# A depthwise convolution's last channel chunk for two more images, computed by ScalarE and GpSimd, and one store of three issued by GpSimd

## The chip, the cores and the metric

The kernel runs on one core of a Trainium2 chip. A core has five engines with an instruction queue each, which run side by side and wait for one another through semaphores: TensorE (PE in the profile; PEld is its weight load) multiplies matrices into PSUM, VectorE (DVE) and ScalarE (ACT) do elementwise work, GpSimd (POOL) does elementwise work on SBUF, and SyncE (SP) only issues transfers. A transfer can be issued by SP, ACT or POOL; it stands in that engine's queue, in order, with everything else that the engine does.

The metric is the device time of one execution in microseconds. Before the change it is 3717.47 us, the median of three runs (3716.41 to 3720.61).

## The reference

The network has four residual layers on an image batch of 8 x 384 channels x 32 x 32 pixels in float32. Each layer adds its result to its input, which it first group-normalises (32 groups). The change concerns the first part of layer 0:

```python
def _dwproj(x, dw, g, b, pw):
    C = x.shape[1]
    y = lax.conv_general_dilated(x, dw, (1, 1), ((1, 1), (1, 1)), feature_group_count=C, ...)
    y = jax.nn.gelu(_bn(y, g, b), approximate=False)
    return jnp.einsum('oc,bchw->bohw', pw, y)
...
q = _dwproj(x, dw_q, g_q, b_q, pw_q).reshape(B, heads, hd, N)
k = _dwproj(x, dw_k, g_k, b_k, pw_k).reshape(B, heads, hd, N)
v = _dwproj(x, dw_v, g_v, b_v, pw_v).reshape(B, heads, hd, N)
```

So three depthwise 3 x 3 convolutions are made of every normalised image, one each for q, k and v: every channel is convolved by itself with nine weights. `_bn` takes mean and variance of each convolved channel over the whole batch, so that no image can go on to the attention before all eight are convolved. Then follow the attention of layer 0, a mixture of experts (layer 1), a ternary-weight convolution (layer 2) and a deformable attention (layer 3). The change leaves those alone.

## The kernel before

**Layout.** Channel 3p + c of an image is on partition p in chunk c (KC = 3 chunks of P = 128 partitions), with 1024 pixels along the free dimension.

**Stage A** is the block under `with ExitStack() as pa` (L217 to L449). For each image b:

- `norm(b)` (L248) group-normalises it in three steps, which are put into three successive turns of the work loop. `begin` takes statistics on VectorE (L103) and joins them (L108). `middle` sends a small matmul through TensorE (L114) and copies it back on VectorE (L116). `end` does a second small matmul (L125), VectorE's L127, a power on GpSimd (L95) and VectorE's L130; then ScalarE writes the three normalised chunks into a padded image `pads[b % 2]` (L144). For some images VectorE copies chunk 2 of it to `xn` (L268).
- `stack(b, g)` (L311) builds TensorE's operand for one group of channels. A group has 42 channels, and its tile has 126 rows: each channel three times, shifted by one image row each. SP issues three SBUF-to-SBUF transfers for it (L318). There are nine such groups in an image (three in each chunk), plus one small group of the last six partitions (index NGC).
- The work loop (from L362) takes one group a turn. Six matmuls (in the profile two instructions each, so 12) convolve it for q, k and v at once into two PSUM banks; ScalarE copies each bank to `y` (L397), VectorE takes its batch statistics (L398), and the three parts of `y` are stored to DRAM, one each for q, k and v (L406). ScalarE's queue issues these stores, except those of the last image's groups 5, 6 and 7, which GpSimd's queue issues.

**What is taken off TensorE already.** For the images in `ON_V` (0, 2, 4, 6) the three large groups of chunk 2 are left out of TensorE's work. `convolve(b, xn)` (L275) computes that chunk on VectorE instead: for each of q, k, v a product with the centre weight (L290) and eight multiply-adds (L292), each over the 126 x 961, 992 or 1024 elements that a shift leaves, and then `finish` (L294): two statistics (L297), one 504 KB store on ScalarE's queue (L298) and three small moves of the statistics on SP's (L300). These 30 steps stand in a list `taps`, from which each turn of the work loop takes two.

**The order.** There are 68 turns: 7 for images 0, 2, 4, 6 and 10 for 1, 3, 5, 7. Within a turn the program order is: the norm's step if one is due, the stacks of up to nine turns ahead (AHEAD), the matmuls with their copies and statistics, the three stores, then the two taps. Every engine keeps to this order in its own queue. The turn at which each image's norm begins comes from `begins` (L341); the next image's load is issued there too.

**Buffers.** Images lie in a pool `im` of five slots, taken in rotation. `st` has ten slots, `y` nine (shared by the groups' results and VectorE's products), and PSUM four banks, two for each group.

**After stage A** the batch statistics are joined and turned into scales (to L449), the first image's convolved q, k, v are loaded from DRAM (`load_b(0)`, issued at the last image's group 5), and ScalarE's first gelu (L494) opens the attention.

Of the kernel before, what the change touches and what calls it, by code (L numbers as in the profile page):

```python
# [13 lines left out]
N = H * W  # L14
# [38 lines left out]
def tile_kernel(ctx: ExitStack, tc: tile.TileContext, i: dict, out: bass.AP):  # L53
# [144 lines left out]

    im = ctx.enter_context(tc.tile_pool(name="im", bufs=5))
# [8 lines left out]
    ON_V = (0, 2, 4, 6)  # L208
# [8 lines left out]
    with ExitStack() as pa:  # L217
# [28 lines left out]
        vst = wa.tile([3 * GC, 3, 2, 6], F32, name="vst")  # L246

        def norm(b):  # L248
# [12 lines left out]
            def end():  # L261
# [4 lines left out]
                if b in ON_V:  # L266
                    xn = wa.tile([3 * GC, H, W], F32, tag="xn", name=f"xn{b}", bufs=2)
                    nc.vector.tensor_copy(xn, pads[b % 2][: 3 * GC, KC - 1, 1 : H + 1, :])  # L268
                    taps.extend(convolve(b, xn))
                for c in range(KC):  # L270
                    moments(xmv[:, b, c, :], state["st"][:, 2 * c : 2 * c + 2, :])
# [3 lines left out]
        def convolve(b, xn):  # L275

            state = {}

            def tap(v, t):
                dy, dx = t // 3 - 1, t % 3 - 1  # L280
                w = cwv[: 3 * GC, v, t : t + 1]
                if t == 4:
                    state["y"] = ya.tile([3 * GC, N], F32, tag="y", name=f"yv{b}_{v}")
                y = state["y"].rearrange("p (h w) -> p h w", h=H)
# [4 lines left out]
                if t == 4:  # L289
                    nc.vector.tensor_scalar(d, f, w, None, ALU.mult)  # L290
                else:
                    nc.vector.scalar_tensor_tensor(d, f, w, d, ALU.mult, ALU.add)  # L292

            def finish(v):  # L294
                y = state["y"]
                for h in range(2):
                    nc.vector.bn_stats(vst[:, v, h, :], y[:, h * HALF : (h + 1) * HALF])  # L297
                nc.scalar.dma_start(out=raw[v][b, : 3 * GC, KC - 1, :], in_=y)  # L298
                for t in range(3):
                    nc.sync.dma_start(  # L300
                        out=cst[v : 3 * GC : 3, 3 * (KC - 1) + t, 2 * b : 2 * b + 2, :],
                        in_=vst[t : 3 * GC : 3, v, :, :],
# [3 lines left out]
            for v in range(3):  # L306
                steps += [lambda v=v, t=t: tap(v, t) for t in (4, 0, 1, 2, 3, 5, 6, 7, 8)]
                steps.append(lambda v=v: finish(v))
            return steps
# [26 lines left out]
        groups = [(NGC, *range(NGC - 3 if b in ON_V else NGC)) for b in range(B)]  # L336
# [4 lines left out]
        begins = {max(2, work.index((b, NGC)) - AHEAD - 2): b for b in range(1, B)}  # L341
        sts, taps, todo, later, normed = {}, [], {}, list(work), {0}
# [21 lines left out]
        for n, (b, g) in enumerate(work):  # L364
# [34 lines left out]
            for v in range(3):  # L399
# [5 lines left out]
                queue = nc.gpsimd if b == B - 1 and g in (5, 6, 7) else nc.scalar  # L405
                queue.dma_start(out=to, in_=of)  # L406
            for _ in range(2):
                if taps:
                    taps.pop(0)()
            if b == B - 1:  # L410
# [3 lines left out]
        assert not taps and not todo and not xts  # L414
# [1509 lines left out]
```

## Time and profile before

| | |
|---|---|
| median of three runs | 3717.47 us |
| the profiled execution's own time | 3716.66 us |
| its span, first to last instruction | 3714.9 us |
| PE busy over the span | 3598.4 us (97%) |
| DVE busy | 1810.6 us (49%) |
| ACT busy | 1273.6 us (34%) |
| POOL busy | 195.9 us (5%) |
| first large matmul of stage A starts | 18.0 us |
| last statistics of stage A (L398) end | 384.4 us |
| first gelu of the attention starts (L494) | 390.2 us |
| PE, DVE, ACT, POOL busy from 0 to 385 us | 352.75, 267.86, 105.40, 18.33 us |
| mean granted TensorE clock from 0 to 385 us | 0.96 |

How to read it: a row of the profile names the line, the engine, the operation, and the tile written and read, with shapes and a count. Then come its busy time, the mean of one in ns, the engine's idle time just before such instructions, and what ended that idle time. Instructions that only issue a transfer are not counted as busy, though they hold their queue: ACTq and SPq rows show them. Matmuls overlap in their pipeline, so the mean of one is longer than their spacing.

### The profile page before, as it was taken

How to read it: one execution, taken by the hardware profiler on the slowest of the kernel's cores; microseconds unless marked ns; L12 is line 12 of the kernel's file. 1: busy time of each engine (PE TensorE's matmuls, PEld its weight loads, DVE VectorE, ACT ScalarE, POOL GpSimd, SP SyncE). 2: the span in 40 equal slices, each digit the busy share in tenths (PEclk: the TensorE clock that was granted, in tenths of full speed). 3: DMA queues.
4: the chain of work that ended last, by engine and by line, in shares of the span. 5: the costliest groups of instructions: out<-in, count | busy, mean ns of one | idle time of the engine just before them, and what ended most of it. 6: DMA issues, size and time to landing. Idle time of an engine off the chain costs nothing.

```text
span 3714.9 us, 39037 instructions
## 1 busy us (share of the span) xinstructions
PE 3598.4 (97%) x15587; PEld 1504.2 (40%) x15587; DVE 1810.6 (49%) x2827; ACT 1273.6 (34%) x1524; POOL 195.9 (5%) x162
## 2 busy tenths in 40 slices
PE   7999999999999999999799999999999999999888
PEld 3444333333333333333244444444344444444433
DVE  6776223232323232323336557564764657557564
ACT  2222354545444453544222321323222232322222
POOL 0000100000000000000000010100101010010111
PEclk9999999999999999999899999999999999999898
DMA  6776311121212021212350010110101001010000
GB/s 205 240 249 231 127 55 36 63 56 43 63 40 78 25 75 28 72 28 72 125 201 23 33 51 20 46 42 33 37 23 56 26 33 43 27 51 20 0 34 18
DMA packets 88178, 253.32 MB, mean 68 GB/s; under 512 B 19114, under 2 KB 19706, under 8 KB 87602
## 3 DMA queue, kind: packets, MB, share of 16 engines
q1 hardware_dynamic: 74904, 211.26, 17.1%
q10 hardware_dynamic: 12504, 37.88, 3.0%
q8 instruction: 127, 2.08, 0.2%
q0 software_dynamic: 576, 1.55, 0.1%
q14 instruction: 67, 0.55, 0.0%
HBM read 133.39 MB, written 75.59 MB: 56 GB/s over the span
## 4 chain that ended last, share of the span: by engine, by line
PE 39%; DVE 10%; ACT 1%; issue 1%; DMA 0%; POOL 0%; DVEq 0%; ACTq 0%; POOLq 0%; SPq 0%
PE y L1295 11%; PE ph L1274 8%; DVE y L1370 6%; PE pq L1415 3%; PE pf L1694 3%; PE pw L1378 3%; PE s L1589 3%; PE pav L1605 2%; DVE hd L1260 1%; PE pss L1631 1%; PE pk L1563 1%; PE pv L1572 1%; DVE off L1485 1%; PE xsb L1549 1%; PE px L1438 1%
## 5 line engine op out<-in xcount | busy, mean ns | idle before, releaser
L645 ACT ACTIVATE p<-s 128x1024 f32<-128x1024 f32 x512 | 496.5, 1021 | 507.0 <-PE s L638 506.7
L1295 PE MATMUL y<-hd,w_sb 128*128 128x512 f32 x1080 | 493.1, 600 | 3.5 <-DVE hd L1260 3.5
L653 PE MATMUL pav<-p,vt 64*64 64x512 f32 x4096 | 487.1, 590 | 0.0
L1274 PE MATMUL ph<-h,w_sb 128*128 128x512 f32 x1104 | 484.1, 594 | 0.4 <-DMA w_sb<-in_w_dram 0.4
L638 PE MATMUL s<-qk,qk 48*64 48x512 f32 x3072 | 370.8, 597 | 3.3 <-ACT p L645 3.3
L391 PE MATMUL pk<-st,cw_sb 126*126 126x512 f32 x720 | 320.3, 606 | 12.7 <-DMA st<-pad 10.9
L1274 PEld LDWEIGHTS ph<-h,w_sb 128*128 128x128 f32 x1104 | 207.5, 190 | 259.5 <-issue 255.3
L1295 PEld LDWEIGHTS y<-hd,w_sb 128*128 128x128 f32 x1080 | 198.0, 191 | 248.4 <-issue 238.2
L653 PEld LDWEIGHTS pav<-p,vt 64*64 64x64 f32 x4096 | 156.6, 133 | 285.1 <-issue 285.1
L610 DVE COPY ta<-pav 128x512 f32<-128x512 f32 x64 | 44.3, 692 | 429.0 <-PE pav L653 426.0
L1284 ACT ACTIVATE hd<-ph,b_sb 128x512 f32<-128x512 f32 x180 | 122.6, 681 | 371.3 <-PE ph L1274 371.2
L1370 DVE SCALAR_TENSOR_TENSOR y<-h,tap,y 128x961 f32<-128x961 f32 (+1 forms) x192 | 234.1, 1244 | 0.6
L391 PEld LDWEIGHTS pk<-st,cw_sb 126*126 126x126 f32 x720 | 139.3, 196 | 185.5 <-issue 179.5
L1485 DVE SCALAR_TENSOR_TENSOR off<-q,dw_sb,off 128x225 f32<-128x225 f32 (+3 forms) x432 | 212.3, 549 | 1.7
L638 PEld LDWEIGHTS s<-qk,qk 48*64 48x64 f32 x3072 | 108.7, 133 | 231.1 <-issue 192.0
L78 DVE COPY qk<-pq 128x512 f32<-128x512 f32 x48 | 33.2, 692 | 292.8 <-PE pq L572 292.8
L397 ACT COPY y<-pk 126x512 f32<-126x512 f32 (+1 forms) x136 | 76.2, 583 | 249.2 <-PE pk L391 111.9
L1596 ACT ACTIVATE p<-s 128x1024 f32<-128x1024 f32 x96 | 93.1, 1021 | 169.5 <-PE s L1589 169.4
L1260 DVE TENSOR_TENSOR hd<-hd,cb 128x512 f32<-128x512 f32 x180 | 122.7, 687 | 48.7 <-ACT hd L1284 48.2
L590 PE MATMUL po<-att,wo_sb 128*128 128x512 f32 x288 | 132.8, 615 | 11.6 <-DMA att<-al 11.6
L1378 PE MATMUL pw<-y,upw 128*128 128x512 f32 x288 | 130.5, 606 | 5.0 <-DVE y L1370 5.0
L572 PE MATMUL pq<-g,wq_sb 128*128 128x512 f32 x288 | 131.5, 607 | 2.0 <-ACT g L494 2.0
(286 smaller groups left out, 3870.2 us busy)
## 6 DMA issues: line engine op xcount, KB each, us to landing
g<-raw SPq DMA_DIRECT2D x72, 512.0 KB
st<-pad SPq DMA_DIRECT2D x180, 168.0 KB
raw<-y ACTq DMA_DIRECT2D x171, 168.0 KB
xa<-in_x_dram SPq DMA_DIRECT2D x24, 512.0 KB
xh<-in_x_dram SPq DMA_DIRECT2D x48, 256.0 KB
f<-in_x_dram SPq DMA_DIRECT2D x24, 512.0 KB
f<-o SPq DMA_DIRECT2D x24, 512.0 KB
o<-ot SPq DMA_DIRECT2D x42, 256.0 KB
```

The costliest lines, as they stand in the source:

```text
L391: nc.tensor.matmul(pk[h].rearrange("p (h w) -> p h w", w=W)[: 3 * nch, :, o0 : o0 + c1 - c0], lhsT=lhs, rhs=rhs, start=(k == 0), stop=(k = ...
L572: nc.tensor.matmul(pq, lhsT=w_in[v][:, c, pr * P : (pr + 1) * P], rhs=acts[b][v][:, c, h * HALF : (h + 1) * HALF], start=(c == 0), stop=(c ...
L590: nc.tensor.matmul(po, lhsT=wo0[:, c, m * P : (m + 1) * P], rhs=atts[b][:, c, hs], start=(c == 0), stop=(c == KC - 1),)
L638: nc.tensor.matmul(s[64 * k : 64 * k + 64, j * HALF : (j + 1) * HALF], lhsT=kt[r, k0 : k0 + 64], rhs=qt[r, h * HALF : (h + 1) * HALF], sta ...
L645: nc.scalar.activation(p, s, AF.Exp, scale=scale)
L653: nc.tensor.matmul(pav[k][64 * j : 64 * j + 64, :], lhsT=vts[b % 2][r, kc, 2 * hd : 2 * hd + 2, :].rearrange("p a b -> p (a b)"), rhs=p[r, ...
L1260: nc.vector.tensor_tensor(hd, hd, state["cb"], ALU.mult)
L1274: nc.tensor.matmul(ph, lhsT=w1[:, e, c, dc * P : (dc + 1) * P], rhs=state["h1"][c], start=(c == 0), stop=(c == KC - 1),)
L1295: nc.tensor.matmul(y, lhsT=w2[:, e, dc, m * P : (m + 1) * P], rhs=state[h, k], start=(k == 0), stop=(k == NE * KC - 1),)
L1370: nc.vector.scalar_tensor_tensor(d, f, tap2[:, c, t : t + 1], d, ALU.mult, ALU.add)
L1378: nc.tensor.matmul(pw[h], lhsT=upw2[:, c, m * P : (m + 1) * P], rhs=y[c][:, hs], start=(c == 0), stop=(c == KC - 1),)
L1485: nc.vector.scalar_tensor_tensor(d, f, dw3[:, t : t + 1], d, ALU.mult, ALU.add)
```

## The change

The set `ON_AP` = (1, 3) joins `ON_V`. For images 1 and 3, too, the three large groups of chunk 2 leave TensorE, so that there are 62 turns. Their chunk is convolved by `convolve(b, xn, xp)`: for each tap ScalarE makes the product of the shifted image with the weight, into a tile `m` of which there is one; GpSimd adds it to the result (the centre tap writes the result directly, with no sum). Image copy and results lie in an image slot `xp` of the pool `im`; the copy is made by GpSimd. The statistics of these results stay on VectorE; their store and the three moves are issued by GpSimd. Each `finish` stands three steps later than the last tap of its product, and three empty steps stand before the last one. So an image has 33 steps, in a list `taps_ap`; each turn takes one of them, and every fourth turn two. They come after VectorE's own two taps in a turn.

The second part: of the three stores of every turn, the one for v (index 2) is issued by GpSimd's queue instead of ScalarE's. With fewer turns, the beginnings of the norms are set at least three turns apart.

```diff
-    ON_V = (0, 2, 4, 6)
+    ON_V, ON_AP = (0, 2, 4, 6), (1, 3)
...
-        vst = wa.tile([3 * GC, 3, 2, 6], F32, name="vst")
+        vst = [wa.tile([3 * GC, 3, 2, 6], F32, name=f"vst{k}") for k in range(2)]
+        QUEUES = (nc.scalar, nc.sync), (nc.gpsimd, nc.gpsimd)
...
+                if b in ON_AP:
+                    xp = image(f"xp{b}")
+                    xn = xp[: 3 * GC, 0, :].rearrange("p (h w) -> p h w", h=H)
+                    nc.gpsimd.tensor_copy(xn, pads[b % 2][: 3 * GC, KC - 1, 1 : H + 1, :])
+                    taps_ap.extend(convolve(b, xn, xp))
...
+                if ap:
+                    if t == 4:
+                        nc.scalar.activation(d, f, AF.Identity, scale=w)
+                    else:
+                        m = wa.tile([3 * GC, H, W], F32, tag="tmp", name=f"m{b}_{v}_{t}")
+                        m = m[:, r0:r1, c0:c1]
+                        nc.scalar.activation(m, f, AF.Identity, scale=w)
+                        nc.gpsimd.tensor_tensor(d, d, m, ALU.add)
+                elif t == 4:
...
             def finish(v):
-                y = state["y"]
+                y, (store, move) = state.pop(v), QUEUES[ap]
                 for h in range(2):
-                    nc.vector.bn_stats(vst[:, v, h, :], y[:, h * HALF : (h + 1) * HALF])
-                nc.scalar.dma_start(out=raw[v][b, : 3 * GC, KC - 1, :], in_=y)
+                    nc.vector.bn_stats(vst[ap][:, v, h, :], y[:, h * HALF : (h + 1) * HALF])
+                store.dma_start(out=raw[v][b, : 3 * GC, KC - 1, :], in_=y)
                 for t in range(3):
-                    nc.sync.dma_start(
+                    move.dma_start(
...
+            if ap:
+                for v in range(3):
+                    k = 9 * (v + 1) + v
+                    steps.insert(min(k + 3, len(steps) - 1), steps.pop(k))
+                steps[-1:-1] = [lambda: None] * 3
             return steps
...
-        groups = [(NGC, *range(NGC - 3 if b in ON_V else NGC)) for b in range(B)]
+        groups = [(NGC, *range(NGC - 3 if b in ON_V + ON_AP else NGC)) for b in range(B)]
...
-        begins = {max(2, work.index((b, NGC)) - AHEAD - 2): b for b in range(1, B)}
-        sts, taps, todo, later, normed = {}, [], {}, list(work), {0}
+        begins, n = {}, -1
+        for b in range(1, B):
+            n = max(n + 3, work.index((b, NGC)) - AHEAD - 2)
+            begins[n] = b
+        sts, taps, taps_ap, todo, later, normed = {}, [], [], {}, list(work), {0}
...
-                queue = nc.gpsimd if b == B - 1 and g in (5, 6, 7) else nc.scalar
+                late = b == B - 1 and g in (5, 6, 7)
+                queue = nc.gpsimd if late or v == 2 else nc.scalar
                 queue.dma_start(out=to, in_=of)
             for _ in range(2):
                 if taps:
                     taps.pop(0)()
+            for _ in range(2 if n % 4 == 0 else 1):
+                if taps_ap:
+                    taps_ap.pop(0)()
```

## The prediction

> **What bounds the kernel now.** The change touches only the first stage, the layer-0 convolutions, so I read that stage's own views. First the page's costliest groups (busy us, mean ns of one; then idle before, by releaser):
>
> ```profile
> L391 PE MATMUL pk<-st,cw_sb 126*126 126x512 f32 x720 | 320.3, 606 | 12.7 <-DMA st<-pad 10.9
> L397 ACT COPY y<-pk 126x512 f32<-126x512 f32 (+1 forms) x136 | 76.2, 583 | 249.2 <-PE pk L391 111.9 <-DMA raw<-y 106.7 <-DVE yv L292 14.2
> ```
>
> TensorE hardly ever waits (12.7 us); the evacuating copies wait for it. Then busy time by stretch (window: length, PE, PEld, DVE, ACT, POOL, clock, DMA share, GB/s):
>
> ```profile
> 24.00:60.00 36.00, 32.99 (x75) 13.69 (x74) 25.61 (x42) 9.86 (x15) 0.56 (x1) 0.86 0.67 214
> 60.00:345.00 285.00, 274.60 (x672) 116.49 (x671) 218.99 (x319) 80.91 (x126) 5.86 (x6) 0.96 0.69 228
> 345.00:385.00 40.00, 38.00 (x91) 16.73 (x89) 15.89 (x26) 9.26 (x16) 4.75 (x9) 1.00 0.92 341
> ```
>
> PE is 96% busy in the body: the stage is TensorE's. DVE is second: 25.61 + 218.99 + 15.89 = 260.5 us. POOL is empty. Next, VectorE's groups in 24 to 385 us:
>
> ```profile
> L292 DVE SCALAR_TENSOR_TENSOR yv<-xn,cwv_sb,yv 126x961 f32<-126x961 f32 (+1 forms) x96 | 117.5, 1224 | 1.5
> L398 DVE BATCH_NORM_STATS2 cst<-y 126x6 f32<-126x512 f32 (+1 forms) x136 | 89.2, 681 | 72.0 <-ACT y L397 72.0
> L103 DVE BATCH_NORM_STATS2 st_a<-xa 128x6 f32<-128x512 f32 x42 | 27.0, 681 | 8.7 <-DMA xa<-in_x_dram 8.4
> L268 DVE COPY xn<-pad 126x1024 f32<-126x1024 f32 x3 | 2.1, 689 | 8.3 <-ACT pad L144 8.3
> L130 DVE SCALAR_TENSOR_TENSOR ss_a<-ga_a,ss_a 128x1 f32<-128x1 f32 x7 | 1.1, 157 | 2.9 <-POOL ss_a L95 2.9
> L116 DVE COPY ga_a<-gna_a 128x2 f32<-128x2 f32 x7 | 1.1, 155 | 4.7 <-PE gna_a L114 4.6
> L127 DVE SCALAR_TENSOR_TENSOR ve_a<-gnb_a,ga_a 128x1 f32<-128x1 f32 x7 | 1.1, 151 | 8.2 <-PE gnb_a L125 8.2
> ```
>
> The 72 us on L398 is DVE being ahead and vanishes when it is late. The others, 8.4 + 8.3 + 2.9 + 4.6 + 8.2 = 32.4 us, are round trips of the norms that stay. Last, the timeline: the price of a group, and ScalarE stopped by DVE (the store of a DVE-made product waits in ScalarE's queue, the copy behind it).
>
> ```profile
> 291.37 10.33 PE L391 MATMUL pk<-st,cw_sb 126*126 126x512 f32 x24
> ...
> 39.39 0.39 ACTq L298 DMA_DIRECT2D raw<-yv  x1
> 39.81 0.58 ACT L397 COPY y<-pk 126x512 f32<-126x512 f32 x1 [8.80 <-DVE yv L292]
> ```
>
> And the issue of stores by ScalarE and by GpSimd (ns min/median/max):
>
> ```profile
> L406 ACTq DMA_DIRECT2D raw<-y x195: 275/774/2223, 26.0 to 385.3; - x195
> L406 POOL DMA_DIRECT2D raw<-y x9: 505/505/756, 369.8 to 379.9; - x9
> ```
>
> [...] The trace agrees, in layer 3:
>
> ```profile
> 2160.05 2.35 POOL L1620 TENSOR_TENSOR p<-p,p 128x1024 f32<-128x1024 f32 x1 [1.89 <-ACT p L1596]
> 2160.53 0.25 DVE L1638 RECIPROCAL rec<-ts 128x16 f32<-128x16 f32 x1
> 2160.82 2.13 DVE L1639 TENSOR_TENSOR tu<-tu,rec 128x512 f32<-128x512 f32 x1
> ```
>
> and over the whole run (ns min/median/max):
>
> ```profile
> L1639 DVE TENSOR_TENSOR tu<-tu,rec x48: 679/1955/2140, 2160.8 to 3694.0; 128x512 f32<-128x512 f32 x48
> ```
>
> The reciprocal (one input) ran its 0.25 us inside POOL's product; the two-input product, 0.68 us alone, took 2.13 and ended 0.55 after POOL let go. L292 is a two-input form too, L398 is not. [...]
>
> **The change, part by part.**
>
> Removed: 6 groups (3 each of images 1 and 3). PE: 72 matmuls x 10.33/24 = 0.430 us = 31.0 us, on the path. ACT: 12 copies x 0.583 = 7.0. SP: 18 stack loads. DVE: 12 statistics x 0.681 = 8.2, given back by 12 new ones on the new products: net zero.
>
> Moved: of ACT's 195 store issues 118 stay (59 groups x 2): -77 x 0.774 = -59.6 us on ACT. POOL gets 59 more x 0.505 = 30 us, plus 6 stores and 18 small moves (some 12 us). Bytes fall a little; DMA share is 0.69, no bound.
>
> Added on ACT: 54 products, 961 to 1024 wide; L144, the same function from SBUF, takes 1.23 for 1024, so about 1.2: +65 us. ACT's sum is unchanged (-7.0 - 59.6 + 65). Its work: 124 x 0.583 + 118 x 0.774 + 65 + 24 x 1.23 + 12 x 0.7 = 267 us of some 329. The 14 groups with two steps can make ACT wait for POOL, since the product buffer is single: at most 1.2 + 2.25 each, 48 us. That still fits.
>
> Added on POOL: 48 sums. From 0.563 (192 wide, three of L1545 undisturbed in 1.69 us on the timeline) to 2.35 (1024) the slope is 2.15 ns per element: 2.21 for 961, 2.28 for 992, mean 2.25 us (estimate from these rows), 108 us in all; two copies of at most 2.35. About 155 us of 330. Behind POOL's instructions stand the norms' powers (0.55 to 0.9 us), for which DVE waits, and the third stores, which hold the y buffers (nine, 6.5 us landing).
>
> Added, the lock: 66 steps at 1.25 per group run from group 4 to group 56 of 62, exactly where DVE has its own taps (to group 59). The price b per sum: nothing if DVE is waiting or in statistics; a full 2.25 - 0.14 = 2.1 us if the next thing on DVE is a tap. In place, ACT does two copies, two issues (1.55) and a product (1.2), so the sum comes about 2.8 us after the second copy. A DVE on time has then just ended two statistics and two taps: b = 0. A DVE one phase late has two statistics (1.2) ahead: b = 0.9. The second sum of a double step meets a tap: b = 2.1. Sums arriving at random would give about 1.5 in a group's work, some 1.1 with norms and waits counted. I take 1.0; ends 0 and 2.1.
>
> Moved in time: norms of images 2 to 7 begin at groups 5, 10, 17, 24, 34, 41. Image 1's working tile is one of five image slots; image 6's load, at group 24, is the one to reuse it, so it waits in SP's queue for the finish at group 29, with stacks from group 33 behind it. Landing 6.5 us, 1.5 MB at some 220 GB/s 7 us: 0 to 7 us of stall, covered if DVE is the later anyway.
>
> The sum. TensorE alone: on the timeline the stage's last L398 ends at 384.4; 384.4 - 31.0 = 353. VectorE alone: 24 + 260.5 + 32.4 = 317, + 48 b. So b up to (353 - 317)/48 = 0.75 is free; at b = 1.0 DVE ends at 365. I add 4 us for hand-overs (SP's hold, ACT's stores behind late taps): 369. The stage shortens by 15.5 us; nothing later changes. The profiled execution took 3716.66 us, 1.8 over its span, 0.8 under the median: 3716.66 - 15.5 = 3701.
>
> **Rivals.**
>
> Hidden lock (0.17): sums settle where DVE is idle or in statistics, b at most 0.75; 353 to 358, a gain of 26 to 31, about 3688. For it: the on-time phase gives zero. Against: seven norms put DVE late (PE already waits for them). Here belongs ACT as bound: 24 + 267 + 48 + some 20 of its norm waits = 359, about 3691.
>
> No change (0.14): b near 1.4, where 317 + 48 b = 384; within 0.2% (7.4 us, about what a measurement of this kernel can tell from no change).
>
> Slower (0.24), one mechanism: lock on L292. From b = 1.4 DVE needs longer than before; at 1.75, 401 + 4 = 405, some 3738; at 2.1, 418, 3750 or more. For it: L1639's median is 1.955 where alone it takes 0.68, and two of three DVE microseconds in a group are taps. Against: two statistics per group always offer cover.
>
> It doesn't do what it says: POOL could be starved instead (DVE wins each time), making ACT wait for the product buffer; this ends near the ACT case, and is counted there.
>
> **How the numbers follow.** Forecast 0.45 (gain 8 to 25: 3692 to 3709), the rest as above. Faster 0.17 + 0.45 = 0.62. Range 3685 to 3739: it leaves out a tail below the hidden case (0.04) and half of the slower case (0.12).
>
> **What would show it.** L391 x648 at the same mean; L292 unchanged in count but longer, mean 1.22 + 1.0 x 48/96 = about 1.7 us, maxima of 3.3; L398 without the 72 us of waits; POOL's sums at 2.3 or longer; the first gelu of the next stage some 15 us earlier than 390.2; PE waits for norms above before. L292's mean under 1.5 would speak for the hidden lock, above 2.0 for the slower case. I am wrong in mechanism if the stage shrinks while L292 is stretched by over 67 us, or fails to shrink with L292 unchanged.

## The result, and the profile after

The kernel after takes 3759.74 us (median; 3758.52 to 3765.05), where before took 3717.67 on the same chip: the ratio is 1.0115, 95% interval 1.01 to 1.0131. The forecast was 3701, with a range of 3685 to 3739 and a chance of 0.24 for slower. So it failed in sign and in size, by 59 us.

The profiled execution has a span of 3757.4 us, 42.5 more than before. Nearly all of it lies ahead of the first gelu, which starts at 432.3 us instead of 390.2; from there to the end both kernels take the same (3325.1 and 3324.7 us). Of these 42.1 us, 32.6 come before the last statistics of stage A (417.0 instead of 384.4), and 9.5 between these and the gelu (15.3 instead of 5.8).

In the new file TensorE's matmul is L419 (before L391), the evacuating copy L425 (L397), its statistics L426 (L398), the stores L435 (L406), VectorE's taps L311 (L292), the moves of its statistics L319 (L300), the stacks L343 (L318). First the same groups of the page as before:

```profile
L419 PE MATMUL pk<-st,cw_sb 126*126 126x496 f32 (+1 forms) x648 | 309.1, 638 | 24.5 <-DMA st<-pad 12.7
...
L311 DVE SCALAR_TENSOR_TENSOR yv<-xn,cwv_sb,yv 126x961 f32<-126x961 f32 (+1 forms) x96 | 149.1, 1553 | 1.0
```

The 72 matmuls are gone (720 to 648), but the mean of one rose from 606 to 638 ns, so that TensorE's busy time fell by only 11 us, and its idle time ahead of them doubled. Busy time by stretch (window: length, PE, PEld, DVE, ACT, POOL, clock, DMA share, GB/s):

```profile
24.00:60.00 36.00, 30.67 (x69) 12.15 (x68) 26.91 (x45) 13.64 (x18) 7.16 (x9) 0.88 0.66 221
60.00:345.00 285.00, 234.54 (x532) 97.94 (x533) 219.59 (x272) 115.35 (x149) 148.22 (x112) 0.87 0.58 188
345.00:385.00 40.00, 40.00 (x91) 16.52 (x90) 34.80 (x39) 12.71 (x19) 16.27 (x15) 0.91 0.65 207
```

In the body, TensorE was busy 274.60 of 285 us before, at a clock of 0.96; now it is 234.54, at 0.87. No other engine has taken its place: VectorE is busy as long as before there (219.59 against 218.99), ScalarE 115 us, GpSimd 148. VectorE does need more in all: 302.3 us from 24 to 418 us, where it was 260.5 from 24 to 385. From the first large matmul to the last statistics, before and after:

```profile
18.00:384.40 366.40, 351.58 (x844) 149.53 (x844) 260.43 (x385) 100.61 (x157) 11.17 (x16) 0.96 0.72 240
...
17.70:417.00 399.30, 342.19 (x772) 142.78 (x772) 303.54 (x382) 149.90 (x199) 178.08 (x149) 0.89 0.61 202
```

TensorE idles 57.1 us of it instead of 14.8. So the stage lost about 33 us in this way: 31 us of matmuls are gone, those that stay take some 22 us more, and 42 us of idling are added (an estimate from these sums). The stage has become one of waits. VectorE's, ScalarE's and GpSimd's groups from 24 to 418 us:

```profile
L307 POOL TENSOR_TENSOR xp<-xp,m 126x961 f32<-126x961 f32 (+1 forms) x48 | 122.2, 2545 | 52.2 <-ACT m L306 52.2
L426 DVE BATCH_NORM_STATS2 cst<-y 126x6 f32<-126x512 f32 (+1 forms) x123 | 81.1, 680 | 68.5 <-ACT y L425 68.4
L306 ACT ACTIVATE m<-xp,cwv_sb 126x961 f32<-126x961 f32 (+1 forms) x48 | 53.3, 1110 | 50.9 <-POOL xp L307 47.1 <-issue 2.7 <-DMA raw<-y 1.1
L130 DVE SCALAR_TENSOR_TENSOR ss_a<-ga_a,ss_a 128x1 f32<-128x1 f32 x7 | 7.2, 1034 | 5.4 <-POOL ss_a L95 5.4
L118 DVE TENSOR_TENSOR dm_a<-mv_a,ga_a 128x1 f32<-128x1 f32 x7 | 7.1, 1021 | 0.1
```

The taps are stretched by 149.1 - 117.5 = 31.6 us, unevenly: half of them still take 1.23 us or less, the longest 3.87. The norms' operations on one element per partition are stretched as well: L118 and L130 took 0.157 us each before, and now 1.02 and 1.03 on the mean. VectorE still waits 68 us for ScalarE's copies, so it was not late throughout. What TensorE and ScalarE wait for, from the list of waits in 0 to 430 us (total us, times, longest):

```profile
PE gna_a L114 <- DVE mv_a L108: 46.2, 6, 16.4
PEld gna_a L114 <- ACT xp L302: 25.0, 2, 17.2
ACT m L306 <- POOL xp L307: 47.1, 21, 4.2
```

The first of these was 14.2 us before (in both, 9.0 us are the first image's norm, ahead of the first group): TensorE stands longer at the norms' small matmul, behind which the groups stand in its queue. The second is the wait of the weight load for that matmul, and overlaps the first. The timeline shows one such place in full (start, length, then in brackets the idle time before and its releaser):

```profile
98.56 0.55 POOL L317 DMA_DIRECT2D raw<-xp  x1 [0.30 <-POOL xp L307]
...
100.63 3.90 DVE L311 SCALAR_TENSOR_TENSOR yv<-xn,cwv_sb,yv 126x992 f32<-126x992 f32 x2
...
104.45 3.65 DVE L103 BATCH_NORM_STATS2 st_a<-xa 128x6 f32<-128x512 f32 x6
106.59 1.15 ACT L302 ACTIVATE xp<-xp,cwv_sb 126x1024 f32<-126x1024 f32 x1 [7.20 <-DMA raw<-xp]
...
108.61 0.56 PE L114 MATMUL gna_a<-mv_a,g_sb 128*128 128x2 f32 x2 [16.45 <-DVE mv_a L108]
...
109.03 7.30 PE L419 MATMUL pk<-st,cw_sb 126*126 126x512 f32 x12
...
113.96 2.20 DVE L119 TENSOR_TENSOR dm_a<-dm_a 128x1 f32<-128x1 f32 x1
```

VectorE's two taps at 100.63 take 3.90 us in place of 2.44, the norm's statistics follow them, and TensorE stands for 16.45 us. ScalarE stands for 7.20 us meanwhile: its third centre tap writes into the slot of the first product, whose store GpSimd has just issued, and must wait until that has landed. Nothing behind it in ScalarE's queue is evacuated, and by the list TensorE's weight load waits for this tap too, until shortly before VectorE is done.

Most of this gap is not the convolution's, though. It stands at the norm of image 3; the same place in before, and in e7 (a run below that has none of the added work):

```profile
104.79 0.35 PE L114 MATMUL gna_a<-mv_a,g_sb 128*128 128x2 f32 x2 [2.45 <-DVE xmv L141]
...
105.25 0.56 PE L114 MATMUL gna_a<-mv_a,g_sb 128*128 128x2 f32 x2 [13.70 <-DVE mv_a L108]
```

In after this norm comes 3.8 us later than in before, but TensorE has come to it 10.2 us sooner (at 92.16 instead of 102.34), since three groups of image 1 are gone. Image 3 isn't there sooner: its load stands in SP's queue behind stacks and three moves of statistics, and is issued at 92.64 us in before, 95.21 in e7 and 96.86 in after. Whether an earlier load would help was not tried.

After the gap TensorE needs 7.30 us for a group of 12, where 24 took 10.33. The trace shows its clock meanwhile: TensorE stops at 92.16; the clock granted is 1.00 from 92 to 96 us, 0.50 from 96 to 113 and 0.99 from 113 to 117. The group begins at 109.03, so it has 4 us at half the clock, worth 2 us; it costs 2.1 us more than its 5.17. In the body the mean clock is 0.87. So this stall of 16.45 us cost 2.1 us more than its length.

Last, the end of the stage:

```profile
406.14 9.33 SPq L169 DMA_DIRECT2D g<-raw  x9
...
416.88 6.53 SPq L319 DMA_DIRECT2D cst<-vst  x3
...
425.60 1.48 DVE L154 BATCH_NORM_AGGREGATE bnmv_qkv<-cst 126x2 f32<-126x96 f32 x3 [8.57 <-DMA cst<-vst]
```

The last three moves of image 6's statistics (VectorE's products) stand in SP's queue behind nine loads of the next stage. Before, they were issued at 356.27 us, ahead of these loads. Now the joining of the statistics waits for them (8.57 us).

One statement ahead of the prediction was wrong: that every engine keeps to the program's order. The compiler's planner orders each engine's instructions anew. In after, ScalarE runs a centre tap and five products in a row between 106.59 and 124.24 us with no evacuating copy among them, where the text has two copies in every turn and at most two products. The text's order had entered the working as a premise.

### The profile page after: what moved, and what is told of

The parts are those of the page before. It is cut to its first block, busy times and chain, and to the rows that moved or that the text cites. A ratio compares the mean times of both kernels' runs of the same rounds, so it can differ in the third digit from the quotient of the medians.

```text
span 3757.4 us, 39094 instructions
## 1 busy us (share of the span) xinstructions
PE 3585.2 (95%) x15515; PEld 1497.0 (40%) x15515; DVE 1854.7 (49%) x2827; ACT 1323.6 (35%) x1566; POOL 363.2 (10%) x295
## 3 DMA queue, kind: packets, MB, share of 16 engines
q1 hardware_dynamic: 73896, 208.16, 16.7%
## 4 chain that ended last, share of the span: by engine, by line
PE 39%; DVE 10%; ACT 1%; issue 1%; DMA 0%; POOL 0%; DVEq 0%; ACTq 0%; POOLq 0%; SPq 0%
PE y L1327 11%; PE ph L1306 8%; DVE y L1402 6%; PE pq L1447 3%; PE pf L1726 3%; PE s L1621 3%; PE pw L1410 3%; PE pav L1637 2%; DVE hd L1292 1%; PE pss L1663 1%; PE pk L1595 1%; PE pv L1604 1%; PE xsb L1581 1%; DVE off L1517 1%; PE px L1470 1%
## 5 line engine op out<-in xcount | busy, mean ns | idle before, releaser
L419 PE MATMUL pk<-st,cw_sb 126*126 126x496 f32 (+1 forms) x648 | 309.1, 638 | 24.5 <-DMA st<-pad 12.7
L419 PEld LDWEIGHTS pk<-st,cw_sb 126*126 126x126 f32 x648 | 131.7, 207 | 194.1 <-issue 176.2
L311 DVE SCALAR_TENSOR_TENSOR yv<-xn,cwv_sb,yv 126x961 f32<-126x961 f32 (+1 forms) x96 | 149.1, 1553 | 1.0
L1292 DVE TENSOR_TENSOR hd<-hd,cb 128x512 f32<-128x512 f32 x180 | 122.2, 684 | 48.6 <-ACT hd L1316 48.3
L1652 POOL TENSOR_TENSOR p<-p,p 128x1024 f32<-128x1024 f32 x48 | 113.2, 2358 | 330.4 <-ACT p L1628 294.3
```

The costliest lines, as they stand in the source:

```text
L419: nc.tensor.matmul(pk[h].rearrange("p (h w) -> p h w", w=W)[: 3 * nch, :, o0 : o0 + c1 - c0], lhsT=lhs, rhs=rhs, start=(k == 0), stop=(k = ...
L1292: nc.vector.tensor_tensor(hd, hd, state["cb"], ALU.mult)
```

## The experiments

What a transfer waits for needs a word first, since several runs turn on it. Each transfer in the trace names the semaphore it raises when it has landed. In before's trace the 528 transfers that SP and ScalarE issue up to 385 us raise the same eight, 65 to 67 each, and of the 520 that raise one again, 510 wait for that same semaphore before they are issued; GpSimd's nine raise eight others. So a stack on SP's queue waits for stores of ScalarE's that use no data of its own (27 times, 41.8 us in all, in the first row below). "Distance" below is the mean number of groups by which a stack is ahead of the store that it has to wait for in this way: 5.9 in before, 4.5 in after. It is the author's own count in the order that the planner made, and takes the eight to be given out in turn there. That order is not in the traces; counted in their order of issue, over the stacks that stand directly behind a store, the mean is lower (5.1 in before, 4.0 in after, 3.6 in e3) and ranks the runs in nearly the same way. SP's waits for ScalarE's stores, in the list of its own waits, before:

```profile
SPq L318 <- DMA raw<-y: 41.8, 27, 6.8
```

and after:

```profile
SPq L343 <- DMA raw<-y: 91.6, 29, 9.1
SPq L343 <- DMA raw<-yv: 40.0, 6, 17.4
```

The last row, 11.5 us before, is for the stores of VectorE's products, which ScalarE can issue only when VectorE is done with them.

All runs, each against before on the same chip (median us of before 3719.9 to 3720.9), with the end of the last statistics in the profiled execution:

| run | median us | ratio, 95% interval | distance | last statistics us |
|---|---|---|---|---|
| e1_floor | 3739.31 | 1.0058 (1.0041 to 1.0074) | 4.3 | 393.9 |
| e2_conv_only | 3753.36 | 1.0086 (1.0069 to 1.0103) | 9.3 | 422.5 |
| e3_store_only | 3764.63 | 1.0120 (1.0104 to 1.0137) | 3.9 | 433.1 |
| e4_order_after | 3753.67 | 1.0084 (1.0067 to 1.0101) | 8.5 | 418.2 |
| e5_order_write | 3748.19 | 1.0080 (1.0064 to 1.0097) | 9.4 | 413.4 |
| e6_before_extra | 3746.99 | 1.0069 (1.0052 to 1.0086) | 5.9 | 411.9 |
| e7_floor_stores_back | 3700.68 | 0.9939 (0.9921 to 0.9957) | 7.0 | 369.5 |
| e8_late_moves | 3752.38 | 1.0089 (1.0072 to 1.0106) | | 412.3 |
| e9_conv_write | 3736.10 | 1.0045 (1.0028 to 1.0062) | 9.3 | 402.2 |
| e10_conv_noprod | 3754.93 | 1.0094 (1.0077 to 1.0111) | 7.2 | 422.0 |
| e11_order_before | 3733.71 | 1.0038 (1.0023 to 1.0052) | 7.8 | 403.7 |
| e12_order_store | 3759.72 | 1.0108 (1.0091 to 1.0124) | 4.0 | 429.1 |
| e13_drop_store | 3752.63 | 1.0088 (1.0071 to 1.0105) | 3.9 | 417.5 |
| e14_tiny_on_gpsimd | 3723.05 | 1.0007 (1.0000 to 1.0014) | 5.9 | 388.0 |
| e15_order_store_far | 3754.54 | 1.0093 (1.0076 to 1.0110) | 5.5 | 421.1 |
| e16_vector_five | 3719.27 | 0.9999 (0.9988 to 1.0009) | 6.9 | 386.3 |
| e17_before_far | 3738.92 | 1.0049 (1.0036 to 1.0062) | 8.7 | 402.8 |
| e18_five_far | 3728.87 | 1.0023 (1.0013 to 1.0033) | 8.8 | 401.0 |

### The two parts of the change, each alone

**e1_floor**, after without any of the added work:

```diff
-                    xn = xp[: 3 * GC, 0, :].rearrange("p (h w) -> p h w", h=H)
-                    nc.gpsimd.tensor_copy(xn, pads[b % 2][: 3 * GC, KC - 1, 1 : H + 1, :])
-                    taps_ap.extend(convolve(b, xn, xp))
+                    nc.gpsimd.memset(xp, 0.0)
+                    for v in range(3):
+                        nc.gpsimd.dma_start(out=raw[v][b, : 3 * GC, KC - 1, :], in_=xp[: 3 * GC, v, :])
```

> The changed kernel without any step for images 1 and 3: no products, no sums, no statistics of their last chunk; GpSimd writes zeros into the slot and stores it, three stores for each image. So the output is not the reference's. Theory [...]: TensorE's own saving stands alone, 3717 - 31 = 3686 +- 6, no PE wait for the norms above before's. Rival (the earlier, closer norms or the third store on GpSimd spoil the stage by themselves): above 3705.

It took 3739.31: 18 us slower than before, with 31 us of matmuls and all of the new work left out. So something other than products and sums costs time.

**e2_conv_only**, after with all three stores of a group on ScalarE again:

```diff
-                queue = nc.gpsimd if late or v == 2 else nc.scalar
+                queue = nc.gpsimd if late else nc.scalar
```

> The changed kernel with all three stores back on ScalarE's queue. Theory (sums on GpSimd hold VectorE): still slower than before, 3750 to 3775, since ScalarE gets 59 more issues of 0.77 us. Rival (the store on GpSimd is the cause): 3700 to 3717.

3753.36: the convolution on ScalarE and GpSimd, too, is slower than before without the moved stores, by 32 us.

**e3_store_only**, before with the third store on GpSimd's queue:

```diff
-                queue = nc.gpsimd if b == B - 1 and g in (5, 6, 7) else nc.scalar
+                queue = nc.gpsimd if v == 2 or b == B - 1 and g in (5, 6, 7) else nc.scalar
```

> The kernel before with only the third store moved to GpSimd's queue. Theory: within 0.2% of before, 3710 to 3725, since GpSimd has nothing else to do. Rival (the store on GpSimd is the cause): 3735 or more.

3764.63: the moved store alone costs 44 us, more than the whole change. In TensorE's waits from 0 to 385 us:

```profile
PE pk L391 <- DMA st<-pad: 28.6, 6, 7.1
PE gna_a L114 <- DVE xmv L141: 22.3, 3, 8.4
```

The first was 10.9 before and the second 2.5. Stacks and norms come late, though ScalarE has become free: it waits 225 us for TensorE and 13 us for its own stores' landing, where before it was 112 and 107.

**e7_floor_stores_back** is e1 with e2's edit: none of the added work, all stores on ScalarE.

> As e1_floor (no products and no sums for images 1 and 3, their last chunk filled with zeros, so the output is not the reference's; 72 matmuls fewer), but all three stores of a group on ScalarE again. A stack stands 7.0 groups behind the store whose completion it needs, against 4.3 in e1_floor. Theory 1 (e1_floor lost TensorE's saving because of the moved store): TensorE's 31 us appear, 3685 to 3700. Theory 2 (the shorter stage is bound by something else, as ScalarE's issues or SP's queue): 3710 to 3740, as e1_floor or a little below.

3700.68 (3691.11 to 3701.52), 19.5 us faster than before and 39 faster than e1, just above the 3685 to 3700 of the first theory. In both places, with and without the groups of images 1 and 3, moving the third store costs about 40 us (of e1's 39, some 10 are the tail after the last statistics, which is 15.6 us there and 5.9 in e7).

With e7, e1, e2 and after, all four combinations of the two parts are measured, all with the shorter TensorE work: neither 3700.68, the moved store alone 3739.31, the convolution alone 3753.36, both 3759.74. So the costs do not add up: 39 and 53 us alone, 59 together. With the convolution there, the moved store costs only 6 to 10 us more (10 when each run is set against before on its own chip), and these lie in the tail: the last statistics end at 422.5 us in e2 and at 417.0 in after. Either part alone is enough to spoil the gain.

e7 also measures what TensorE's shorter work can bring at best. Its row in the stage:

```profile
L419 PE MATMUL pk<-st,cw_sb 126*126 126x496 f32 (+1 forms) x648 | 293.9, 614 | 12.1 <-DMA st<-pad 8.5 <-ACT y L425 3.1 <-DVE ve_a L127 0.5
```

The busy time falls by 26.4 us, but the stage ends only 14.9 us earlier: TensorE now waits 28.8 us for the norms' L108, where it was 14.2 (before, then e7, in 0 to 385 us):

```profile
PE gna_a L114 <- DVE mv_a L108: 14.2, 3, 9.0
...
PE gna_a L114 <- DVE mv_a L108: 28.8, 4, 13.7
```

The 13.7 us are the gap at image 3's norm.

### Why the convolution costs 53 us (e2 against e7)

**e9_conv_write**, e2 with fills in place of the sums:

```diff
-                        nc.gpsimd.tensor_tensor(d, d, m, ALU.add)
+                        for _ in range(3):
+                            nc.gpsimd.memset(m, 0.0)
```

> The kernel of e2_conv_only (all three stores on ScalarE; products and sums for images 1 and 3), with each of GpSimd's 48 sums replaced by three fills of the product buffer: ScalarE's 51 products and the chain between ScalarE and GpSimd stay, nothing on GpSimd reads SBUF. The sums are left out of the computation (the output is not the reference's). e2_conv_only took 3753.4 and the same kernel without products and sums (e7) 3700.7, so 53 us are to be shared out. Theory 1 (the hold on VectorE while GpSimd reads): most of it goes, 3700 to 3722. Theory 2 (ScalarE's products among the evacuations and the hand-overs): most of it stays, 3738 to 3756. Between: both have a part.

3736.10, between the two. The taps, 1650 ns on the mean in e2, are back at the value they have alone:

```profile
L312 DVE SCALAR_TENSOR_TENSOR yv<-xn,cwv_sb,yv 126x961 f32<-126x961 f32 (+1 forms) x96 | 117.4, 1223 | 1.3
```

GpSimd was as busy (134 us of fills in e9, 125 us of sums in e2), and the fills only write. That the sums' reads hold VectorE, and not something else in which a sum differs from a fill, is the author's reading; the two were not tried apart. Of the 53 us, 17 go with the sums. The other 35 stay with what else e9 has and e7 has not: ScalarE's products and the chain between ScalarE and GpSimd, but also the centre taps, twelve statistics on VectorE and the stores and moves of the results. These were not tried apart.

**e10_conv_noprod**, e2 without the products:

```diff
-                        m = wa.tile([3 * GC, H, W], F32, tag="tmp", name=f"m{b}_{v}_{t}")
-                        m = m[:, r0:r1, c0:c1]
-                        nc.scalar.activation(m, f, AF.Identity, scale=w)
-                        nc.gpsimd.tensor_tensor(d, d, m, ALU.add)
+                        nc.gpsimd.tensor_tensor(d, d, f, ALU.add)
```

> The kernel of e2_conv_only without ScalarE's 48 products: GpSimd adds the shifted input itself in place of a product, so its 48 sums and their hold on VectorE stay, and ScalarE issues none of them (the weights of 48 products are left out of the computation, so the output is not the reference's). Theory 1 (the hold on VectorE): most of the 53 us between e7 and e2 stays, 3735 to 3755. Theory 2 (ScalarE's products and hand-overs): most of it goes, 3703 to 3722.

3754.93: with the products gone, nothing is won. The sums now run without a pause, and their stretch is worst at the start. In the busy time by stretch of e10, where before had 56.74 us of TensorE in this window:

```profile
60.00:120.00 60.00, 30.53 (x64) 12.41 (x64) 43.48 (x40) 9.97 (x14) 48.62 (x27) 0.73 0.43 132
```

With GpSimd busy 48.6 of 60 us, VectorE comes to 40 instructions where it had 71, and image 3's norm reaches TensorE at 127.0 us instead of 104.8. So each half suffices: sums without products cost 54 us over e7, products with fills 35, products with sums 53. The two do not add up. In all three the norms come later: that of the last image reaches TensorE at 271 us in e7, 288 in e9, 298 in e2 and 307 in e10.

**e4_order_after** is after with ScalarE, VectorE, GpSimd and TensorE kept to the order of the text:

```diff
-        for n, (b, g) in enumerate(work):
+        with tc.manual_schedule(engines={mybir.EngineType.Activation, mybir.EngineType.DVE, mybir.EngineType.Pool, mybir.EngineType.PE}):
+            for n, (b, g) in enumerate(work):
...
```

> The changed kernel, with stage A's instructions on TensorE, VectorE, ScalarE and GpSimd issued in the order of the program text instead of the planner's. Theory A (the planner's order, which puts up to eight products in a row ahead of the evacuating copies, turns the lock into idle TensorE): 3705 to 3730. Theory B (the lock alone, at 1 us a sum or more, is enough): 3750 to 3770.

3753.67: still 33 us slower than before, so the planner's order is not all that ruins the change. **e5_order_write** adds e9's fills to it.

> The kernel after with ScalarE, VectorE, GpSimd and TensorE issuing in the order of the text (as e4_order_after), and each of GpSimd's 48 sums replaced by three fills of the product buffer, which keep GpSimd busy about as long, keep the chain ScalarE product -> GpSimd -> next product, but read nothing from SBUF. The sums are left out of the computation (the output is not the reference's). Theory 1 (VectorE is held while GpSimd reads two operands; about 0.95 us per sum, and the norms' small operations pay it too): VectorE's L311 falls from 1553 to about 1220 ns, TensorE's waits for the norms shrink, and the time falls well below that of e4_order_after (3753.7): 3700 to 3725. Theory 2 (ScalarE's products and the hand-overs between ScalarE and GpSimd delay the evacuations, whatever GpSimd does in its part): 3745 to 3760.

3748.19, on the rival's side. The taps fall from 1406 to 1227 ns, yet TensorE still waits 48.5 us for the norms' L108, against 52.6 in e4. The two times are 5 us apart, which their intervals don't separate. In the text's order, then, the hold on VectorE accounts for little, and the rest stays with the other added work and the order.

**e11_order_before** puts before's engines into the order of the text.

> The kernel before with ScalarE, VectorE, GpSimd and TensorE issuing the stage's work in the order of the text; SP's queue is left to the planner. A stack stands 7.8 groups behind the store whose completion it needs (5.9 in before). It is the control for e12_order_store and for e4_order_after. Theory 1 (the distance sets the time): as before or a little better, 3705 to 3725. Theory 2 (the order of the text is itself costly, from which e4 and e5 suffer too): 3735 to 3755.

3733.71, under the second theory's 3735 by little: the text's order costs 14 us by itself. This qualifies e4 and e5, which carry that loss too. With the text's order in both, the change costs 20 us (e4 against e11) instead of 42; about 10 of these 22 us are the tail, which is 5.8 us in e4. What the planner makes of the change thus has a part in its cost.

### Why the moved store costs 44 us

**e6_before_extra**: before, with the third part stored once more by GpSimd, to a scratch tensor.

```diff
+    extra = dram.tile([B, NGC + 1, GC, N], F32, name="extra")
...
                 queue.dma_start(out=to, in_=of)
+                if v == 2:
+                    nc.gpsimd.dma_start(out=extra[b, g, :nch], in_=of)
```

> The kernel before with one transfer added per group: GpSimd's queue stores the third part of y a second time, to a scratch tensor, while ScalarE keeps all its three stores. The order on SP's and ScalarE's queues stays as before, and a stack still stands 5.9 groups behind the store whose completion it needs. Theory 1 (in e3_store_only the moved store cost 44 us because stacks and image loads came to stand only 3.9 groups behind ScalarE's stores): no change, 3713 to 3730. Theory 2 (transfers on GpSimd's queue are themselves the cost, by their traffic or by GpSimd's work for them): slower as in e3_store_only, 3745 to 3770.

3746.99, which looked like the second theory: slower by 27 us though the distance is unchanged. From a transfer's record and its semaphore the time from the end of its issue to full landing can be read. On the mean, in the first 385 us: a stack takes 3.43 us in before and 3.79 here, a store of ScalarE's 3.50 and 3.94. Some 510 transfers go through the eight semaphores, and 510 x 0.4 / 8 = 26 us (an estimate from these numbers; it takes every transfer to stand in one of eight chains that never pause).

**e14_tiny_on_gpsimd** tells traffic from queue: a transfer of 32 bytes in place of that store.

```diff
+                if v == 2:
+                    fill = wa.tile([1, 8], F32, tag="fill", name=f"fill{b}_{g}", bufs=8)
+                    nc.gpsimd.dma_start(out=fill, in_=y[:1, :8])
```

> The kernel before with one more transfer per group on GpSimd's queue, 32 bytes from y to a spare tile; order and distance as before (5.9). Theory 1 (e6_before_extra lost 27 us because 11 MB more made every transfer of the stage land later: st 3.43 to 3.79 us, raw 3.50 to 3.94 us on the mean, with eight semaphores in turn for about 510 of them, 0.4 x 510 / 8 = 26 us): no change, 3714 to 3730. Theory 2 (GpSimd's issuing, or the y buffers it holds, cost): 3738 to 3755.

3723.05, 2.8 us above before, and as the first theory expected (3.44 and 3.56 us to landing). GpSimd is busy 0.52 us for each of these transfers, as for e6's (0.51), so that its issuing costs next to nothing here. That leaves e6's 27 us to the 11 MB more.

But e3 moves no more bytes than before, and its stacks take 3.08 us, less than before. **e12_order_store** is e11 with e3's edit.

> As e11_order_before, with the third store of each group on GpSimd's queue; the compute engines' order is the same text in both, and only SP's stands closer: 4.0 groups between a stack and the store whose completion it needs, against 7.8 in e11. Theory 1 (that distance is what e3_store_only lost 44 us to): 25 to 50 us above e11_order_before. Theory 2 (e3 lost by the planner's order on the compute engines): within 10 us of e11_order_before.

3759.72, 26 us above e11, in the first theory's range. And **e13_drop_store** takes the third store away altogether:

```diff
+    rd = [raw[0], raw[1], raw[1]]
...
-            load_image(acts[b][v], raw[v][b])
+            load_image(acts[b][v], rd[v][b])
...
+                if v == 2:
+                    continue
                 queue.dma_start(out=to, in_=of)
```

> The kernel before without the third store of each group on any queue; the loads of the third raw tensor read the second instead (the output is not the reference's). The planned order is that of e3_store_only: a stack stands 3.9 groups behind the store whose completion it needs (5.9 in before). 11 MB fewer are stored in the stage, ScalarE issues as in e3, and GpSimd's queue carries nothing more than before. Theory a (the distance costs): 3735 to 3765, near e3_store_only (3764.6), less what the smaller traffic gives back. Theory b (GpSimd's queue or its transfers cost): at or below before, 3690 to 3722.

3752.63. With the store gone from every queue, and 11 MB less to move, the kernel is still 32 us slower than before. SP's wait and TensorE's, in the lists of waits of e13 from 0 to 385 us, are close to those of e3 (78.3, 28.6 and 22.3):

```profile
SPq L319 <- DMA raw<-y: 72.6, 27, 6.7
...
PE pk L392 <- DMA st<-pad: 26.2, 6, 7.1
PE gna_a L114 <- DVE xmv L141: 18.2, 3, 7.3
```

This narrows the cause: neither GpSimd's queue nor the store's traffic is needed for these 32 us. What is left is the order that the planner makes once the third store no longer stands among the others, on SP's and ScalarE's queues or on the compute engines, which e13 shares with e3. e12 against e11, with the text's order on the compute engines in both, still shows 26 us; this speaks for the order of the transfers. The 12 us from e13 to e3 may be the store's own traffic (stacks land after 2.62 us in e13 and 3.08 in e3); that was not tried apart.

Whether the distance itself is what counts in that order was the next question. **e15_order_store_far** adds two tiny transfers per group on ScalarE to e12:

```diff
+                if v == 2:
+                    for k in range(2):
+                        fill = wa.tile([1, 8], F32, tag="fill", name=f"fill{b}_{g}_{k}", bufs=8)
+                        nc.scalar.dma_start(out=fill, in_=y[:1, :8])
```

> The kernel of e12_order_store (third store on GpSimd, text order on the compute engines) with two tiny transfers (32 bytes each) per group added on ScalarE, which move a stack's distance from the store it needs from 4.0 to 5.5 groups. ScalarE issues one transfer per group more than in before. Theory a (the distance costs): nearer to e11_order_before (3733.7) than to e12 (3759.7), 3735 to 3750, though two issues per group are added. Theory b (the store on GpSimd costs by itself): 3757 to 3775.

3754.54 lies between the two ranges. It is 5 us better than e12, with two more issues per group, but their intervals overlap. TensorE's waits for stacks fell from 24.1 to 10.7 us, those for the norms stayed (36.4). **e17_before_far** adds one such transfer to before.

> The kernel before with one transfer of 32 bytes per group added on ScalarE's queue: a stack stands 8.7 groups behind the store whose completion it needs, against 5.9. TensorE's gaps over 1 us in the stage are 16 us in before, and 11 us of its waits are for stacks. Theory a (distance is still worth something at 5.9): 3706 to 3716. Theory b (at 5.9 nothing is left to gain, and 68 issues of 0.77 us on ScalarE are only added): 3718 to 3735.

3738.92, slower by 19 us, a little beyond the second theory's range, which put the cost down to ScalarE's added issues. So more distance alone does not help. But e17 is no clean test of it: the added transfer also shifts who stands behind whom. By the semaphores in the trace 93 of 228 stacks stand directly behind a store in before, and 19 in e17. Which property of the order makes it dear is left open.

### The tail, and whether anything is faster

**e8_late_moves**, after with image 6's nine moves on GpSimd's queue:

```diff
                 y, (store, move) = state.pop(v), QUEUES[ap]
+                if b == 6:
+                    move = nc.gpsimd
```

> The kernel after with the nine moves of image 6's statistics (L319) on GpSimd's queue in place of SP's. Theory 1 (the last three moves stand behind nine image loads in SP's queue and hold the end of the stage by 9.5 us): 3748 to 3753, first gelu at 420 to 424 us. Theory 2 (another wait, as for the loads of g or the last statistics, takes its place): 3756 to 3763.

3752.38, 32 us above before on its chip, where after is 42 above. The tail from the last statistics to the gelu is 5.9 us again (5.8 in before): the late moves did hold it.

**e16_vector_five** takes the three groups of image 1 off TensorE by giving them to VectorE, with all stores on ScalarE and no sum on GpSimd:

```diff
-    ON_V = (0, 2, 4, 6)
+    ON_V = (0, 1, 2, 4, 6)
...
-        begins = {max(2, work.index((b, NGC)) - AHEAD - 2): b for b in range(1, B)}
+        begins, n = {}, -1
+        for b in range(1, B):
+            n = max(n + 3, work.index((b, NGC)) - AHEAD - 2)
+            begins[n] = b
...
-            for _ in range(2):
+            for _ in range(2 + (n % 2)):
```

> The kernel before with the last chunk of image 1 convolved on VectorE too (the chunks of five images there, none on GpSimd, all stores on ScalarE), the norms' steps spaced as in after, and up to three of VectorE's steps per group. TensorE has 36 matmuls fewer (15.5 us), VectorE about 34 us more (27 x 1.22 + 6 x 0.68 less 6 x 0.68 of the groups' own statistics). Distance 6.9. Theory 1 (what hurt in after were the hold, the hand-overs and the moved store, not the work on VectorE): 3703 to 3718. Theory 2 (VectorE's later norms cost more than TensorE saves): 3722 to 3740.

3719.27, the same as before, a point between both ranges. 36 matmuls fewer are repaid by gaps: those of TensorE over 1 us, from the first large matmul to the last statistics, sum to 31.0 us, against 11.6 in before. The longest, 11.44 us, is again at image 3's norm. **e18_five_far** adds e17's transfer.

> As e16_vector_five (3719.3), with one transfer of 32 bytes per group added on ScalarE's queue: distance 8.8 in place of 6.9. Theory a: 3700 to 3714. Theory b: 3718 to 3735.

3728.87: slower, as e17. No version was found that beats before and computes the reference.

## Why the prediction failed, step by step

**TensorE's saving: right in its term, wrong in its worth. This step failed.** The 31.0 us of matmuls were counted onto the path in full. e7, where nothing replaces them, gains 19.5 us at the median, and its stage, in the profiled execution, 14.9. A body in which TensorE is 96% busy is not bound by it alone: image 3's norm, which waits for its load, comes no sooner, and TensorE idles 13.7 us there. The prediction read TensorE's waits from the row of the large matmuls (12.7 us); the norms' small matmul had 16.7 us more in a row of its own (9.0 of them ahead of the first group).

**The lock: right in size.** 48 sums stretched the taps by 31.6 us, L130 by 7.4 - 1.3, L118 by 7.3 - 1.2, and L119 from 0.154 to 0.404 us on the mean of eight, in all some 46 us: 0.95 a sum, where 1.0 was chosen. The choice was made for the taps, though, and on these it is 0.66: in the trace of after the 46 taps that overlap a sum take 1.92 us on the mean, and none of the other 50 over 1.25. A sum that meets statistics was priced at nothing, and that held: the 31 of L426 that overlap one take 0.68 us, as all of them do (0.68 in before). What was not foreseen is the rest: an operation on one element per partition took as long as a whole sum or longer (L118 takes 0.10 us at least and 2.24 at most, L130 up to 2.75), and these stand on the norms' way to TensorE:

```profile
L118 DVE TENSOR_TENSOR dm_a<-mv_a,ga_a x8: 103/160/2237, 9.8 to 310.9; 128x1 f32<-128x1 f32 x8
```

GpSimd's sum, estimated at 2.25 us alone, takes 2.23 at least and 2.30 at the median; its mean of 2.55 is raised by sums that met a tap: of the 18 over 2.35 us, 15 began within 0.6 us after a tap had begun, and of the other 30 one did.

**The sum for the stage: this step failed.** VectorE's end was reckoned as 317 + 48 b, as if its busy time and the norms' round trips decided once it passed TensorE. VectorE is busy 219.59 of 285 us in the body, no more than before, and still waits 68 us for ScalarE; these waits were expected to vanish. TensorE has 42 us more of idling, some 30 of it at the norms' small matmuls, and some 22 us more for the matmuls that stay, at a lower clock. A bound made of one engine's busy time sees neither.

**The 4 us for hand-overs: failed.** ScalarE's wait for the single product buffer was put at up to 48 us that "still fit" on ScalarE. It is 47.1 us, and ScalarE has room for it by its busy time (115 of 285 us in the body). But evacuations and norms stand behind these waits in ScalarE's queue. e9, whose fills leave the taps at their own 1.22 us, is still 35 us above e7; how much of this is the waiting was not tried apart. The wait of the third centre tap for a store's landing (7.20 us at 106.59) was not in the list.

**The moved store: failed.** It was priced at the issuing time it frees on ScalarE (59.6 us) and takes on GpSimd (30 us), and at nothing on the path; this was the author's estimate, which no run had shown. In e14 a tiny transfer per group on GpSimd's queue costs 2.8 us, but e3 costs 44 us, and e13, without that store, 32. This leaves the order of what stays, most likely of the transfers; which property of it is not known. Beside the convolution, as in the change itself, the store adds only 6 to 10 us.

**Nothing later changes: wrong by 9.5 us,** by the moves behind the loads; e8 shows it.

**The rival "slower": right in sign, wrong in mechanism.** It asked for b of 1.4 or more on L292; b was 0.66 there and 0.95 with the norms' small operations. The loss came through the terms above. Of the signs that were listed, the count of 648, the longer taps (1.55 us, named as 1.7; longest 3.87, named as 3.3), sums at about 2.3 us or longer and longer waits for the norms came true; the same mean of L391, an L398 without its 72 us, and an earlier gelu did not.

## What to carry to other kernels

A stage whose first engine is 96% busy can be one pace among two: before counting work taken off it as time, look at what it will come to sooner, and whether that can be ready (here image 3's norm, whose load stands behind stacks). Where a two-input VectorE instruction meets one of GpSimd's like these sums, price it by GpSimd's (here 0.16 us became up to 2.75 beside sums of 2.3) and not by its own size, and look first for tiny ones on a chain. And when an instruction is moved to another queue, ask what order the compiler makes of those that stay; a run with the instruction left out altogether tells whether its cost lies in itself or in what stays. Of a change in two parts, run all four combinations: here either part alone costs most of what both cost.

## What the runs showed of the hardware that had not been expected

- A VectorE operation on 128 x 1 elements with two SBUF inputs takes 0.16 us alone and up to 2.75 us beside GpSimd's sum; fills of the same buffer, as busy on GpSimd, leave VectorE's taps at 1223 ns (e9).
- After a TensorE gap of 16.45 us, twelve matmuls take 7.30 us in place of 5.17; the granted clock is 0.50 from 3.8 us after the gap's beginning to 4 us after the group's. In the body its mean falls from 0.96 to 0.87.
- 11 MB more in a stage that moves some 91 MB in 385 us made the stacks land 0.36 us and ScalarE's stores 0.44 us later on the mean, and the kernel 27 us slower (e6), while a tiny transfer per group on the same queue cost 2.8 us (e14, interval 1.0000 to 1.0014).
